# Another order for the readers of three shared PSUM tiles in a gated-delta-rule block

## The chip, the core and the metric

The kernel runs on one core of one Trainium2 chip. The metric is the device time of one execution in microseconds, lower being better. It was measured three times for the kernel before: 2231.53, 2234.38 and 2236.29 us, a median of 2234.38.

## What is computed

The reference is one transformer block on `x` of 8 sequences with 256 tokens of 256 channels, all in float32: a layer norm with per-sequence scale and shift, an attention layer whose state follows the gated delta rule, a gated residual, a second such norm, and a feed-forward layer of which only the two largest of every four hidden values are kept. The heart is the recurrence, for 16 key heads with two value heads each, all of width 128:

```python
def step(S, inp):
    q_t, k_t, v_t, b_t, d_t = inp
    Sk = jnp.einsum('bhi,bhipj->bhpj', k_t, S)
    dv = b_t[..., None] * (v_t - Sk)
    upd = jnp.einsum('bhi,bhpj->bhipj', k_t, dv)
    S = S * d_t[:, :, None, :, None] + upd
    o = jnp.einsum('bhi,bhipj->bhpj', q_t, S)
    return (S, o)
```

Its input is a projection of the tokens, convolved over four taps; its output is normalised, multiplied by a silu gate and projected back.

## The kernel before

**Tiling.** The sequences are taken in four pairs (`bp`), the key heads in groups of four (`GH`), so there are 16 groups and 64 turns of one head with one pair. The 256 tokens of a sequence are two chunks of 128 (`NCH`). Inside a chunk the recurrence is written as matrix products with the inverse of a triangular 128x128 matrix, for each of 8 systems (2 sequences, 2 chunks, 2 value heads) of a turn.

**Stages.** `prepare` makes query, values and gate of a head: products into PSUM (`ps_qv`, L432, and `ps_z`, L634), the convolution (ScalarE L418 for one tap, VectorE L420 for three more). `stage_a` and `stage_b` make keys, decays and the inverses of the 32x32 blocks for the next group; they run in the background. `levels` puts the 32x32 inverses together to 128x128 in two levels, 64 times in all. `attend` does the recurrence for one head and one sequence, 128 times in all. `shares` multiplies by the output weights (`ps_y`, L890). `feed_forward` of a finished pair of sequences fills in beside the next pair, and the last pair's runs alone at the end.

**The order of the work.** The stages are Python generators that the main loop steps in turn, which gives the program order. The tile framework then makes each engine's queue: a scheduler with a timing simulation of its own (`schedule_with_timeline_sim=True`) may move instructions past each other where no dependency forbids it. So an edit of a few lines can move instructions on every engine for the whole length of the kernel. Each engine runs its own queue strictly in order, and semaphores tie the queues together.

**Shared tiles.** A PSUM tile is one bank. The pools are `ps_in` (3 banks), `ps_inv` (2) and `ps_mix` (3). Two readers of one tile on different engines are put in program order: the later one gets a semaphore wait on the earlier one, although both only read. Readers on the same engine need no such wait. A bank is given to the next tile when its last reader is done. Three tiles matter here.

- `ps_t` in `levels` (products at L705). ScalarE evicts one half of it with a minus sign into `tt` (L712, partitions 64 to 95), VectorE transposes the other half into `low` (L714, partitions 0 to 31), ScalarE copies `low` twice into `x_top` (L720), and evicts the untransposed half last (L726). A DMA on SyncE's queue (L718) moves rows that L712 wrote into `low_up`. TensorE needs `x_top` at L731 and L734, and `low_up` at L745, one step later.
- `ps_kq` in `attend` (L779 to L783). VectorE makes the masked scores `aq` (L785), then ScalarE the two copies of `cross` (L793). TensorE needs `cross` for `ps_ks` (L806) and `aq` for `ps_o` (L824) and later for the second `ps_o` (L836).
- `ps_ks` in `attend` (L806). For each of the two value heads VectorE makes `rr` (L811) and ScalarE a part of the output `o` (L819), in turn: `rr`, `o`, `rr`, `o`. TensorE needs both `rr` for the second `ps_u` (L830). The `o` is wanted only at L837, by VectorE.

Between these, ScalarE copies of `ps_u` to `u` (L800 and L832) feed the next products directly.

## Time and profile before

| what | value |
|---|---|
| median of three runs | 2234.38 us |
| the profiled execution's own time | 2234.34 us |
| its span, first to last instruction | 2232.6 us |
| around the span | 1.7 us |
| TensorE matmul (PE) busy | 2093.5 us |
| TensorE weight loads (PEld) busy, beside the matmuls | 1643.0 us |
| VectorE (DVE) busy | 1675.3 us |
| ScalarE (ACT) busy | 1366.9 us |
| GpSimd (POOL) busy | 367.1 us |
| mean granted TensorE clock | 0.982 |

The profile names for each group of instructions the line, the engine, the tile written and the tiles read. A row of the waits reads "engine, tile and line that waited <- who ended the wait: us in total, times, longest". Matmuls are pipelined and their ends are modelled, so busy time of PE is an upper estimate of its work. Idle time of an engine counts only if TensorE, or another engine at the end of the chain, waits for it.

By stretches, PE is busy 103.1 us of the first 120 us, 1935.8 us of the 2050 us up to 2170 us, and 54.6 us of the last 62.6 us, in which the last pair's feed-forward runs by itself.

### The profile page before, as it was taken

What the parts mean: (1) busy time and instruction counts of PE and PEld (TensorE: products, weight loads), DVE (VectorE), ACT (ScalarE), POOL (GpSimd) and SP (SyncE); (2) the same over time, 40 slices, a digit from 0 to 9 for tenths busy, and PEclk for the clock granted to TensorE, in tenths of its full rate; (3) what the DMA queues carried; (4) which work ended last, traced back from release to release, by engine and by line L of the source; (5) the groups of instructions that cost most, each with busy time, mean ns of one, the idle gap of its engine ahead of it and who ended that gap; (6) DMA issues with size and microseconds to landing.
All of it is one profiled execution on the core that took longest, in us unless ns stands there. A gap on an engine that the chain in (4) does not pass through costs nothing. (4 is left out here: it accounts for less than half of the span.)

```text
span 2232.6 us, 46262 instructions
## 1 busy us (share of the span) xinstructions
PE 2093.5 (94%) x16684; PEld 1643.0 (74%) x16684; DVE 1675.3 (75%) x4039; ACT 1366.9 (61%) x4551; POOL 367.1 (16%) x375
## 2 busy tenths in 40 slices
PE   8899989899999999999999999999999999999998
PEld 5576767677677777777777777777778777777787
DVE  6687676886868696885968778686886869678547
ACT  3586666766656656665666666565665566666552
POOL 3120211212120211211111120221212012120010
PEclk9999999999999999999999999999999999999999
DMA  4332323323233433424333342433424243332336
GB/s 138 87 107 62 101 70 87 89 80 95 81 98 95 117 107 98 118 75 122 104 102 111 115 110 87 114 93 100 128 78 119 76 127 107 105 101 80 77 96 208
DMA packets 324515, 226.83 MB, mean 102 GB/s; under 512 B 254520, under 2 KB 266168, under 8 KB 324288
## 3 DMA queue, kind: packets, MB, share of 16 engines
q1 hardware_dynamic: 304416, 163.34, 27.4%
q10 hardware_dynamic: 19872, 60.54, 8.4%
q8 instruction: 133, 2.18, 0.4%
q14 instruction: 94, 0.77, 0.1%
HBM read 186.28 MB, written 29.12 MB: 96 GB/s over the span
## 5 line engine op out<-in xcount | busy, mean ns | idle before, releaser
L420 DVE SCALAR_TENSOR_TENSOR cv<-ps_qv,conv_sb,cv 128x510 f32<-128x510 f32 (+2 forms) x564 | 413.6, 738 | 72.3 <-ACT cv L418 69.2
L432 PE MATMUL ps_qv<-h_bp,wh 128*128 128x512 f32 x768 | 372.8, 610 | 5.2 <-DVE cv L420 2.5
L105 POOL TENSOR_TENSOR rs<-ss,minus_halves 128x4 f32<-128x4 f32 x128 | 137.6, 1076 | 1111.4 <-DVE ss L847 1107.7
L634 PE MATMUL ps_z<-wh,h_bp 128*128 128x256 f32 x1024 | 254.0, 391 | 6.9 <-ACT junk L451 3.8
L890 PE MATMUL ps_y<-wo,og_p 128*128 128x256 f32 x1024 | 238.8, 383 | 1.9 <-ACT o L819 1.9
L432 PEld LDWEIGHTS ps_qv<-h_bp,wh 128*128 128x128 f32 x768 | 135.3, 194 | 111.8 <-issue 99.2
L634 PEld LDWEIGHTS ps_z<-wh,h_bp 128*128 128x128 f32 x1024 | 190.3, 196 | 36.1 <-ACT junk L451 6.1
L890 PEld LDWEIGHTS ps_y<-wo,og_p 128*128 128x128 f32 x1024 | 189.4, 191 | 29.1 <-ACT o L819 2.2
L844 ACT ACTIVATE junk<-o 128x128 f32<-128x128 f32 x512 | 153.4, 303 | 78.6 <-DVE o L837 74.0
L592 DVE TENSOR_TENSOR tmp<-blk,xb 128x30 f32<-128x30 f32 (+14 forms) x480 | 157.1, 327 | 34.0 <-ACT xb L586 25.0
L551 DVE TENSOR_TENSOR_SCAN e<-dbc,diag 128x1032 f32<-128x1032 f32 x60 | 138.1, 2302 | 48.8 <-POOL diag L516 42.6
L516 POOL TENSOR_TENSOR diag<-consts,bk 128x1032 f32<-128x1032 f32 x64 | 122.9, 1920 | 307.5 <-DVE bk L507 305.8
L418 ACT ACTIVATE cv<-ps_qv,conv_sb 128x512 f32<-128x512 f32 x188 | 129.6, 691 | 67.9 <-PE ps_qv L432 67.0
L860 DVE SCALAR_TENSOR_TENSOR og<-o,rs,gz 128x128 f32<-128x128 f32 x512 | 145.1, 345 | 30.8 <-POOL rs L105 29.2
L598 DVE TENSOR_TENSOR xb<-xb,tmp 128x30 f32<-128x30 f32 (+14 forms) x480 | 156.9, 327 | 10.1
L420 DVE SCALAR_TENSOR_TENSOR k_t<-ps_k,conv_sb,k_t 128x510 f32<-128x510 f32 (+1 forms) x189 | 139.3, 738 | 23.9 <-ACT k_t L418 20.7
L806 PEld LDWEIGHTS ps_ks<-u,cross 128*128 128x128 f32 x1024 | 129.6, 193 | 15.2 <-issue 9.1
L819 ACT ACTIVATE o<-ps_ks,g_in 128x128 f32<-128x128 f32 x256 | 91.5, 367 | 80.0 <-DVE rr L811 78.4
L806 PE MATMUL ps_ks<-u,cross 128*128 128x128 f32 x1024 | 138.9, 279 | 0.7 <-DVE y L901 0.5
L190 PE MATMUL ps_ff<-h,w_ff 128*128 128x128 f32 x1024 | 128.4, 278 | 10.9 <-issue 7.4
L190 PEld LDWEIGHTS ps_ff<-h,w_ff 128*128 128x128 f32 x1024 | 120.9, 192 | 22.8 <-issue 15.2
L432 PE MATMUL ps_k<-h_bp,wk 128*128 128x512 f32 x256 | 123.5, 607 | 1.8 <-ACT junk L451 1.4
(177 smaller groups left out, 4345.4 us busy)
## 6 DMA issues: line engine op xcount, KB each, us to landing
wh<-in_w_heads ACTq DMA_DIRECT2D x64, 640.0 KB, 4.0
w_ff<-in_w_ff SPq DMA_DIRECT2D x128, 256.0 KB, 3.1
dbc<-d_dram SPq DMA_DIRECT2D x60, 516.0 KB, 3.8
wo<-in_w_heads ACTq DMA_DIRECT2D x32, 512.0 KB, 3.7
w_dn<-in_w_down SPq DMA_DIRECT2D x64, 256.0 KB, 3.1
wk<-in_w_keys SPq DMA_DIRECT2D x16, 512.0 KB, 3.2
scr<-a_t SPq DMA_DIRECT2D x256, 32.0 KB, 2.1
blk<-scr SPq DMA_DIRECT2D x16, 512.0 KB, 3.7
```

The costliest lines, as they stand in the source:

```text
L105: nc.gpsimd.tensor_tensor(out=out, in0=in_, in1=minus_halves[:, :n], op=ALU.pow)
L190: nc.tensor.matmul(ps[:, a, l, :], lhsT=w[:, k, l, :], rhs=h2[:, k, :], start=(k == 0), stop=(k == CC - 1),)
L420: nc.vector.scalar_tensor_tensor(out=dst[:, :, d:], in0=ps[:, :, : T - d], scalar=taps[:, KC - 1 - d : KC - d], in1=dst[:, :, d:], op0=ALU ...
L432: nc.tensor.matmul(ps.rearrange("p b t -> p (b t)"), lhsT=w[k], rhs=h_bp[:, k, :], start=(k == 0), stop=(k == CC - 1),)
L551: nc.vector.tensor_tensor_scan(e.rearrange("p i s t -> p (i s t)"), dbc.rearrange("p i f -> p (i f)"), diag.rearrange("p s t -> p (s t)"), ...
L592: nc.vector.tensor_tensor(out=tmp, in0=blk[:, j, j + 1 :, None].to_broadcast([P, m, j]), in1=xb[:, j, None, 0:j].to_broadcast([P, m, j]), ...
L598: solved = nc.vector.tensor_tensor(out=xb[:, j + 1 :, 0:j], in0=xb[:, j + 1 :, 0:j], in1=tmp, op=ALU.subtract)
L634: nc.tensor.matmul(ps[:, n, :], lhsT=h_bp[:, k, i * T + n * P : i * T + (n + 1) * P], rhs=wh[:, k * 640 + 384 : (k + 1) * 640], start=(k = ...
L806: nc.tensor.matmul(ps_ks[:, ct, h, :], lhsT=cross[:, h, ct, :], rhs=u0[:, h, :], start=True, stop=True)
L844: nc.scalar.activation(junk, o[:, n, h, :], AF.Square, accum_out=ss[:, n, h : h + 1])
L860: nc.vector.scalar_tensor_tensor(out=og[:, n, h, :], in0=o[:, n, h, :], scalar=rs[:, 2 * n + h : 2 * n + h + 1], in1=gz[:, i, n, h, :], op ...
L890: nc.tensor.matmul(ps_y[:, n, :], lhsT=og_p[:, j // 2, i, n, j % 2, :], rhs=wo[:, j // 2, j % 2, :], start=(j == 0), stop=(j == 3),)
```

## The change

Three pairs of statements change places. Nothing is added to or taken from the computation; no tile, pool or size changes.

```diff
@@ levels
-            nc.scalar.activation(tt[even[1], :, odd[1]], ps[even[1]], AF.Copy, scale=-1.0)
             low = mixp.tile([Q, NP, Q], F32, tag="low", name="low", bufs=1)
             nc.vector.transpose(
                 low.rearrange("p s t -> p (s t)"),
                 ps[even[0]].rearrange("p s t -> p (s t)"),
             )
+            nc.scalar.activation(tt[even[1], :, odd[1]], ps[even[1]], AF.Copy, scale=-1.0)
             nc.sync.dma_start(out=low_up[0 : 2 * Q], in_=tt[2 * Q :, NS:, 2 * Q :])
@@ attend
+            cross = two.tile([P, 2, 2, P], F32, tag="cross", name="cross")
+            for h in range(2):
+                nc.scalar.activation(cross[:, h], ps_kq[:, 1:3], AF.Copy, scale=e[:, i, h, P:PE1])
             aq = two.tile([P, NCH, 2, P], F32, tag="aq", name="aq")
             nc.vector.tensor_tensor(
                 out=aq,
...
-            cross = two.tile([P, 2, 2, P], F32, tag="cross", name="cross")
-            for h in range(2):
-                nc.scalar.activation(cross[:, h], ps_kq[:, 1:3], AF.Copy, scale=e[:, i, h, P:PE1])
             yield
@@ attend
                     op0=ALU.mult,
                     op1=ALU.add,
                 )
+            for h in range(2):
                 nc.scalar.activation(
                     o[:, 1, h, :], ps_ks[:, 0, h, :], AF.Copy, scale=g_in[rec["bp"]][:, i, h0 + h : h0 + h + 1]
                 )
```

After it, `low` reads `ps_t` ahead of L712's eviction, and the DMA of L718 still follows that eviction; both copies of `cross` read `ps_kq` ahead of `aq`; both `rr` read `ps_ks` ahead of both `o`. Of the built program, the queues differ on every engine over the whole length. TensorE's queue falls into 3304 runs of equal instructions, where it had 3331.

## The prediction

> **What bounds the kernel.** I read the page first, then the waits of TensorE, then all waits, then one stretch of the timeline.

> ```profile
> span 2232.6 us, 46262 instructions
> PE 2093.5 (94%) x16684; PEld 1643.0 (74%) x16684; DVE 1675.3 (75%) x4039; ACT 1366.9 (61%) x4551; POOL 367.1 (16%) x375
> ...
> PE   8899989899999999999999999999999999999998
> ...
> PEclk9999999999999999999999999999999999999999
> ```

> TensorE sets the time: busy 94% in every slice, at nearly its full clock. It does the same products after the change, so the change can act only on its idle time, 2232.6 - 2093.5 = 139.1 us, and on how its queue is ordered. Adding up all rows of TensorE's waits by the engine that ended them, 83 us are ended by ACT, 23 by DVE, 18 by DMAs. These rows touch the three tiles:

> ```profile
> PE ps_gt L876 <- ACT cross L793: 13.5, 9, 3.1
> ...
> PE ps_w L731 <- ACT x_top L720: 5.1, 4, 2.2
> ...
> PE ps_u L798 <- ACT cross L793: 3.5, 3, 2.2
> ...
> PE ps_w L731 <- ACT t_inv L726: 2.1, 6, 0.6
> ...
> PE ps_y L890 <- ACT o L819: 1.9, 2, 0.9
> ...
> PE ps_t L745 <- DMA low_up<-t_inv: 1.2, 1, 1.2
> ...
> PE ps_u L830 <- ACT o L819: 0.6, 1, 0.6
> ...
> PE ps_u L830 <- DVE rr L811: 0.2, 1, 0.2
> ```

> Without the DMA they are 13.5 + 5.1 + 3.5 + 2.1 + 1.9 + 0.6 + 0.2 = 26.9 us, 1.2% of the span: the most that the edits can win directly. `ps_gt` and `ps_u` read no `cross`; they wait because `cross` is the last reader of the bank that they take over. The rest of what the tiles cost lies on ACT and DVE (all waits):

> ```profile
> ACT o L819 <- DVE rr L811: 78.4, 93, 4.1
> ...
> DVE cv L420 <- ACT cv L418: 69.2, 61, 3.9
> ...
> ACT x_top L720 <- DVE low L714: 47.9, 27, 4.9
> ...
> DVE low L714 <- ACT t_inv L712: 22.5, 21, 3.9
> DVE rr L811 <- ACT o L819: 21.6, 32, 1.4
> ...
> ACT cross L793 <- DVE aq L785: 17.2, 17, 4.3
> ...
> ACT u L800 <- PE ps_u L798: 13.4, 13, 2.4
> ```

> Here engines wait for a reader of the same bank, not for data. The timeline shows how such a chain runs (start, duration, engine; idle time in brackets):

> ```profile
> 2160.80 0.35 DVE L811 SCALAR_TENSOR_TENSOR rr<-ps_ks,g_ex,vn 128x128 f32<-128x128 f32 x1 [3.02 <-PE ps_ks L806]
> ...
> 2161.18 0.37 ACT L819 ACTIVATE o<-ps_ks,g_in 128x128 f32<-128x128 f32 x1 [1.41 <-DVE rr L811]
> ...
> 2161.58 0.35 DVE L811 SCALAR_TENSOR_TENSOR rr<-ps_ks,g_ex,vn 128x128 f32<-128x128 f32 x1 [0.43 <-ACT o L819]
> ```

> `rr` ends at 2161.15, `o` starts at 2161.18, ends at 2161.55, and the second `rr` starts at 2161.58: a hand-over costs 0.03 us, and the second `rr`, which TensorE needs, is 0.43 us late for an `o` that nobody needs yet.

> **Part by part.** No instruction is added or removed, so busy times stay; waits move.

> *Both `rr` first.* From the end of `ps_ks` to the second `rr` the least was 0.04 + 0.34 + 0.03 + 0.37 + 0.03 + 0.34 = 1.15 us (means of L811 and L819: 340 and 367 ns) and becomes 0.04 + 2 x 0.34 = 0.72. In the queues of the two built programs the waits of `o` on DVE fall from 256 to 128 and those of `rr` on ACT from 128 to none. Directly TensorE can win the 1.9 + 0.6 + 0.2 = 2.7 us of `ps_y` and `ps_u` (L830), of which `ps_y` waits for a bank whose last reader stays `o`. I take half: **-1.4**, bounds 0 and -2.7. The remaining `o` wait comes 0.34 us later in the chain, so I count half of the 78.4 us of ACT as freed: 39.

> *`cross` first.* `cross` now waits for the products alone, which frees 17.2 us of ACT. From `ps_kq` to the second `cross` the least falls from 0.04 + 0.68 + 0.03 + 2 x 0.49 = 1.73 to 1.02 us; to `aq` it rises from 0.72 to 1.02 + 0.03 + 0.68 = 1.73. In TensorE's order at least 3.4 us of other products lie between `ps_kq` and the `ps_o` that needs `aq`, and 12.7 at the median, so the later `aq` costs nothing by itself; without that cover it would be 1.0 us in each of 128 turns. The bank is given back after all three readers as before, now by DVE. Of the 17.0 us in which TensorE waited for that bank, I take a quarter as won, nearer to nothing, because the chain to the bank's release is as long as it was: **-4.2**, bounds -17.0 and, where DVE's queue is the later one, about the same the other way, +17.0.

> *ACT freed.* 39 + 17.2 = 56 of ACT's idle 850 us (2232.6 - 1366.9, less what lies below the threshold of a wait) go. TensorE's ACT-ended waits outside the three tiles are 83 - 27 = 56 us. In proportion, 56/850 x 56: **-3.7**, bounds 0 and twice that.

> *DVE.* Its waits for `rr` (21.6) and `low` (22.5) go, 44 us. New are the waits of `aq` for `cross`. The nearest row is DVE reading behind ACT in `ps_qv`: 69.2 us over 188 such pairs, so 47 us over 128. At the other end all 128 wait the whole pair, 130 us. I take 47, which cancels the 44: **0**. Behind a waiting `aq` in DVE's queue stand convolutions (L420), which give `ps_in` banks back to TensorE; at 130 us, TensorE's 23 us of DVE-ended waits grow in proportion to DVE's 554 idle us by 86/554 x 23 = 3.6, or threefold if convolutions bear it all, +11.

> *`low` first.* ACT's queue has L712, L720, L720, L726 in this order before and after. The two chains to `x_top` are 0.04 + 0.375 + 0.03 + 0.43 + 0.03 + 0.62 and 0.04 + 0.43 + 0.03 + 0.375 + 0.62: the same but 0.03 us. Only `low` is earlier, and L712 is 0.47 us later with all that depends on it: the DMA of L718, queued on SP, which lands 2.2 us after its issue. TensorE waited for it once (1.2 us) and it has a whole step of `levels` as cover, so **+1**; all 64 uncovered would be 64 x 0.47 = +30. Behind it on SP stand mostly the transfers of the next turn's `x_top` (35 of 64), which have a whole turn, some 35 us (2232.6/64), and wait 0.47 us longer. DVE's 22.5 us go, ACT's 47.9 move from L720 to L712.

> The 22.5 us of `low` waiting for L712 are a row of this case. [...]

> *TensorE's order.* The scheduler moves products on the whole length. I compared the four links in which one ACT copy stands between two products, `u`, second `u`, `w1` and `w2`, by the products that lie between, at the spacing of the trace (0.111 us for 128 columns, 0.434 for 512). The least hop is 0.03 + 0.37 + 0.03 = 0.43 us; with one ACT instruction of 0.5 ahead 0.95. Links with less cover than that, before and after: first `u` to `ps_ks` 3 and 11 of 128, second `u` to `ps_o` 20 and 16 of 128, `w1` 3 and 1 of 64, `w2` 6 and 1 of 64. The missing cover adds up to 12.2 us before and 9.3 after: **-3**; with hops of 1.5 us 32.1 and 29.0, again -3. The first `u` alone gets worse, by 3 to 10 us; the others win 6 to 13. Fewer runs in the queue (3331 to 3304) at 139/3331 us of idle each are 1 us, within this.

> Sum: -1.4 - 4.2 - 3.7 + 0 + 1 - 3 = -11.3. The profiled execution took 2234.34 us, which is the median of the runs (2234.38). So **2223.0 us**.

> **Rivals.**
> 1. *More is won* (0.12). All 26.9 us and the freed ACT's 3.7 go: 2203.7. For it: the waits of TensorE are long (3.1 us) where ACT's head is blocked. Against: of 27 us, 7.2 hang on a chain (`x_top`) that is not shortened.
> 2. *Nothing to be measured* (0.19): the ACT waits were idle time that nobody needed, and only +1 and -3 remain, or `aq` takes on DVE what ACT got free (-11.3 + 11): 2232 to 2234. For it: TensorE waits for `rr` only 0.2 us in all.
> 3. *Slower, through the first `u`* (0.27). 28 of 128 copies have under 1.5 us of products as cover, where 10 had; ACT stood ready for this copy only 13 times of 128, so it usually has others ahead. If hops are 1.5 us and the gains on the other links and banks stay on paper, it is 2234.3 + 9.7 = 2244; hops of 2 us cost 18.2 and make it 2252. It decides from hops of 1.2 us on (5.2 us), if nothing else is won.

> **How the numbers follow.** The forecast has 0.42, the rivals 0.12, 0.19 and 0.27. A difference of 0.2% (4.5 us) is about what a measurement of this kernel can tell from no change. Faster by more: 0.42 + 0.12 = 0.54; within: 0.19; slower: 0.27. The forecast's own range is 2216 to 2230. The range to be held 8 times in 10 goes from the most that can be won, 2204, to rival 3 with hops of 2 us, 2252; what lies beyond on either side, such as `low_up` uncovered in all turns, I give under 2 in 10.

> **What would show it.** Right: the row of `o` waiting for `rr` falls to about half, those of `rr` for `o`, `cross` for `aq` and `low` for L712 are gone; a row of `aq` waiting for `cross` appears with some 50 us; PE's idle time is some 11 us less, with `ps_gt` <- `cross` replaced by a smaller row. ACT's wait at L720 turns into one at L712 of like size. Wrong: PE waits for `u` or `w` of over 10 us, `aq` waiting for over 100 us with `ps_qv` waiting for `cv`, or `ps_t` (L745) waiting for the DMA in many turns. A granted clock other than 0.98 would move the time by itself and would have to be taken out first.

## The result and the profile after

The changed kernel took 2275.51 us (median of 5 runs, 2271.46 to 2276.57), the kernel before 2233.97 us beside it (5 runs): a ratio of 1.0184, 95% interval 1.0169 to 1.0198. It is 1.8% slower. The forecast, 2223.0 us with 2204 to 2252, was wrong in sign and in range.

The page of the kernel after, its span and its sums (lines behind L818 are one higher than before; the moved statements are now at L713, L717, L786 and L788):

```profile
span 2274.8 us, 46446 instructions
...
PE 2109.9 (93%) x16684; PEld 1649.2 (72%) x16684; DVE 1680.2 (74%) x4039; ACT 1352.9 (59%) x4549; POOL 374.1 (16%) x375
```

The span is 42.2 us longer: TensorE is idle for 164.8 us where it was 139.1 (+25.7), and it is busy for 16.4 us more with the same 16684 products. The second part is the clock. The mean granted clock fell from 0.982 to 0.974. In the clock records it drops to 0.5 for pieces of 3.41 or 6.83 us: 22 pieces before, 27 after. Within the span that is 81.9 and 117.7 us at half speed, so 41.0 and 58.9 us lost. Busy time less that loss is 2052.6 before and 2051.0 after. This profile has the lowest clock of the five runs: the other four show 0.977 and 0.978, which is some 50 to 52 us lost, so the clock's part there is 9 to 11 us in place of 17.9. Two stretches of equal length, before and then after (start and end, length, busy time of PE, PEld, DVE, ACT, POOL with counts, PEclk, DMA share, GB/s), show the loss on the whole length:

```profile
500.00:1000.00 500.00, 474.29 (x3796) 372.87 (x3795) 391.93 (x932) 314.03 (x1080) 85.47 (x85) 0.99 0.35 97
1000.00:1500.00 500.00, 474.35 (x3948) 376.41 (x3946) 383.69 (x900) 304.02 (x1028) 83.68 (x82) 0.99 0.39 109
```

```profile
500.00:1000.00 500.00, 467.31 (x3792) 365.63 (x3792) 376.02 (x885) 299.78 (x1034) 85.90 (x82) 0.98 0.34 95
1000.00:1500.00 500.00, 472.81 (x3844) 371.18 (x3842) 376.32 (x872) 300.61 (x1042) 85.99 (x83) 0.98 0.37 104
```

PE is busy for less of both stretches and at a slightly lower clock. The same products of `attend` (`ps_kq`, `ps_ks`, `ps_o`) come 7 to 9 us late at 500 us, 16 at 1000, 29 to 35 at 1500 and 40 at 2100. So the loss has no one place; it gathers over the whole length.

TensorE's waits, before and then after:

```profile
PE ps_z L634 <- ACT junk L451: 3.8, 7, 0.8
...
PE ps_qv L432 <- DVE cv L420: 2.5, 4, 1.1
...
PE ps_out L244 <- DMA w_dn<-in_w_down: 2.1, 3, 1.2
...
PE ps_u L798 <- ACT og_p L877: 1.4, 3, 0.5
```

```profile
PE ps_u L798 <- ACT og_p L878: 13.3, 12, 1.6
PE ps_out L244 <- DMA w_dn<-in_w_down: 12.7, 8, 4.6
PE ps_qv L432 <- DVE cv L420: 11.9, 7, 3.6
PE ps_z L634 <- ACT junk L451: 11.4, 8, 1.9
PE ps_gt L877 <- DVE aq L788: 9.8, 13, 1.4
```

The row of `ps_gt` waiting for `cross` (13.5) is replaced by a smaller one, for `aq` (9.8), as forecast. What grew stands on other tiles. `junk` (L451) is a sum of squares by ScalarE over `ps_n2q` or `ps_n2k`, banks of the pool `ps_in` that `ps_z` and `ps_qv` also use; `og` is the gated output that VectorE makes, `ps_gt` its transpose by TensorE and `og_p` ScalarE's copy of that. By the engine that ended them, TensorE's waits for ACT fell from 83.3 to 72.0 us, those for DVE rose from 23.1 to 56.1 and those for DMAs from 18.4 to 27.9.

All waits after, the rows of the three tiles:

```profile
ACT t_inv L717 <- DVE low L713: 61.7, 24, 6.0
...
ACT o L820 <- DVE rr L811: 44.5, 39, 3.9
...
ACT t_inv L717 <- DVE rstd L134: 35.6, 6, 7.0
...
DVE aq L788 <- ACT cross L786: 12.5, 26, 1.1
```

`o` for `rr` fell from 78.4 to 44.5; the rows of `rr` for `o`, `cross` for `aq` and `low` for L712 are gone; `aq` waits for `cross` for 12.5 us in all. The eviction, now at L717, waits for `low` and also sits behind `rstd`, other work of VectorE. So on its own tiles the change did what was forecast, at a lower price in waits, and the time was lost elsewhere.

### The profile page after: what moved, and what is told of

The parts are those of the page before. It is cut to its first block, busy times and chain, and to the rows that moved or that the text cites. A ratio compares the mean times of both kernels' runs of the same rounds, so it can differ in the third digit from the quotient of the medians.

```text
span 2274.8 us, 46446 instructions
## 1 busy us (share of the span) xinstructions
PE 2109.9 (93%) x16684; PEld 1649.2 (72%) x16684; DVE 1680.2 (74%) x4039; ACT 1352.9 (59%) x4549; POOL 374.1 (16%) x375
## 2 busy tenths in 40 slices
PE   8899989899999999999999999999999999999998
## 5 line engine op out<-in xcount | busy, mean ns | idle before, releaser
L420 DVE SCALAR_TENSOR_TENSOR cv<-ps_qv,conv_sb,cv 128x510 f32<-128x510 f32 (+2 forms) x564 | 413.3, 738 | 83.8 <-ACT cv L418 80.2
L432 PE MATMUL ps_qv<-h_bp,wh 128*128 128x512 f32 x768 | 372.4, 609 | 15.3 <-DVE cv L420 11.9
L105 POOL TENSOR_TENSOR rs<-ss,minus_halves 128x4 f32<-128x4 f32 x128 | 144.6, 1130 | 1061.6 <-DVE ss L848 1060.7
L634 PE MATMUL ps_z<-wh,h_bp 128*128 128x256 f32 x1024 | 261.2, 398 | 26.7 <-ACT junk L451 11.4
L592 DVE TENSOR_TENSOR tmp<-blk,xb 128x30 f32<-128x30 f32 (+14 forms) x480 | 156.4, 326 | 38.2 <-ACT xb L586 29.5
L418 ACT ACTIVATE cv<-ps_qv,conv_sb 128x512 f32<-128x512 f32 x188 | 129.0, 688 | 93.1 <-PE ps_qv L432 92.7
L420 DVE SCALAR_TENSOR_TENSOR k_t<-ps_k,conv_sb,k_t 128x510 f32<-128x510 f32 (+1 forms) x189 | 138.8, 736 | 33.6 <-ACT k_t L418 32.0
L806 PEld LDWEIGHTS ps_ks<-u,cross 128*128 128x128 f32 x1024 | 130.1, 192 | 18.5 <-issue 9.6
L806 PE MATMUL ps_ks<-u,cross 128*128 128x128 f32 x1024 | 139.8, 278 | 1.1
L772 ACT ACTIVATE vn<-ps_v,nk 128x256 f32<-128x256 f32 x256 | 108.3, 474 | 18.6 <-PE ps_v L767 17.7
```

Of the source, the lines that this page charges most:

```text
L105: nc.gpsimd.tensor_tensor(out=out, in0=in_, in1=minus_halves[:, :n], op=ALU.pow)
L420: nc.vector.scalar_tensor_tensor(out=dst[:, :, d:], in0=ps[:, :, : T - d], scalar=taps[:, KC - 1 - d : KC - d], in1=dst[:, :, d:], op0=ALU ...
L432: nc.tensor.matmul(ps.rearrange("p b t -> p (b t)"), lhsT=w[k], rhs=h_bp[:, k, :], start=(k == 0), stop=(k == CC - 1),)
L592: nc.vector.tensor_tensor(out=tmp, in0=blk[:, j, j + 1 :, None].to_broadcast([P, m, j]), in1=xb[:, j, None, 0:j].to_broadcast([P, m, j]), ...
L634: nc.tensor.matmul(ps[:, n, :], lhsT=h_bp[:, k, i * T + n * P : i * T + (n + 1) * P], rhs=wh[:, k * 640 + 384 : (k + 1) * 640], start=(k = ...
L806: nc.tensor.matmul(ps_ks[:, ct, h, :], lhsT=cross[:, h, ct, :], rhs=u0[:, h, :], start=True, stop=True)
```

## The experiments

Two theories stood against each other; the expectations name them R and Q (two more, P and I, are told in theirs). **R (readers):** one of the new orders of readers costs by itself, above all `aq` behind `cross`. **Q (queues):** the edit only makes the scheduler write other queues, and these happened to be worse; any edit could do so. Each ratio is to the kernel before on the same chip, with its 95% interval.

### One order of queues, the other order of readers

The first four kernels hold each engine's queue to the order that the other kernel's has, by ordering edges without a semaphore between neighbours of a queue (those that float keep only their own dependencies):

```diff
+        for a, b in zip(queue, queue[1:]):
+            tc.add_manual_dep(b, a.name, NoSync, reason="queue")
```

`e1_old_queues`: the statements of after, the queues of before; only `o` and L717 float.

> The changed kernel's statements, so the three tiles are read in the new order, but the queues of TensorE, VectorE, GpSimd and SyncE are held to those of the kernel before, and ScalarE's too but for the 256 `o` and the 64 evictions of L712, which may float. Theory Q (the loss of 42 us comes from the queues that the scheduler made anew, not from the readers): 2215 to 2238 us, that is the prediction's own -11 or nothing; TensorE's idle about 125 to 140 us. Theory R (the readers' new order itself costs, banks coming free later and `aq` holding VectorE's queue): 2265 to 2276 us with the old queues as well.

Measured: 2399.03 us, 1.0755 [1.0731, 1.0779]. Its waits:

```profile
DVE aq L788 <- ACT cross L786: 204.8, 103, 5.9
...
PE ps_gt L877 <- DVE og L861: 68.7, 36, 4.2
```

`aq` keeps its early place in DVE's queue and must now wait there for `cross`, with the rest of that queue behind it: 204.8 us, in place of the 12.5 of the changed kernel, where the scheduler was free to move it.

`e2_new_queues`: the statements of before, the queues of after; `o`, `aq` and L712 float.

> The other corner: the statements of the kernel before, so the tiles are read in the old order, but the queues held to those of the changed kernel, only `o`, `aq` and the eviction of L712 floating. Theory Q: 2262 to 2295 us, the loss stays although the readers stand as before (or grows, since these queues were not made for them). Theory R: 2230 to 2245 us, the loss goes with the readers.

Measured: 2387.47 us, 1.0703 [1.0681, 1.0724]. Here it is the second `rr` that stands too early for its reader order:

```profile
DVE rr L811 <- ACT o L819: 99.8, 127, 2.9
```

Both times lie far above what either theory expected. Both show that an order of readers and a queue belong together, and neither weighs R against Q. So all readers of the three tiles (`o`, `rr`, `aq`, `cross`, `low`, the eviction) were left to float in the next two.

`e9_old_queues_free_readers`: the statements of after, the queues of before but for the readers.

> As the first run with held queues, but all readers of the three tiles (`o`, `rr`, `aq`, `cross`, `low` and L712) may float on ScalarE and VectorE; all else is held to the queues of the kernel before. In that first run `aq` was held at its old place and made VectorE wait 205 us for `cross`. Theory P (a reader needs its own place in its engine's queue, and the first run held it in the wrong one): most of the 168 us go, 2225 to 2280 us, with `aq` waiting under 60 us. Theory Q (the loss of the whole change comes from TensorE's and the other queues): 2215 to 2245 us. Theory R (the readers' order itself costs): 2260 us or more.

Measured: 2248.99 us, 1.0083 [1.0053, 1.0113].

`e10_new_queues_free_readers`: the statements of before, the queues of after but for the readers.

> The other corner again: the statements of the kernel before, all readers of the three tiles free, all else held to the queues of the changed kernel. Theory P: far below the 2387 us of the run that held `rr` too, since `rr` no longer waits for `o` with the queue held. Theory Q: 2260 to 2295 us. Theory R: 2225 to 2250 us.

Measured: 2322.39 us, 1.0412 [1.0379, 1.0445]. In before's queues the kernel with the new readers is 0.8% slower than the kernel before. In after's queues it is the old order that is worse, by 1.0412 / 1.0184 = 2.2% against the changed kernel. So queues fit the readers that they were written for. The first came between the range of Q (to 2245 us) and that of R (from 2260), as the third theory of its text, P, had it (2225 to 2280, `aq` waiting for under 60 us: it waited for 10.4); the second came above Q's and R's. How the 1.8% divides between R and Q these two don't show: no kernel was run that is held to its own queues, so what the holding itself costs is unknown.

### Each part alone, and in pairs

Each kernel has one or two of the three hunks shown in the change, and nothing else.

```diff
 e3: cross ahead of aq                   (hunk 2)
 e4: both rr ahead of both o             (hunk 3)
 e5: low ahead of the eviction           (hunk 1)
 e11: hunks 2 and 3;  e13: hunks 1 and 3;  e14: hunks 1 and 2
```

> `cross` ahead of `aq` alone, queues as the scheduler makes them. Theory R: this part frees its bank by VectorE and holds VectorE's queue, so it should carry most of the loss: 2260 to 2276 us. Theory Q: any value within some 2% of 2234 us, above or below, with no relation to the whole change.

> Both `rr` ahead of both `o` alone. Theory R: it only removes waits, so 2225 to 2236 us. Theory Q: any value within some 2% of 2234 us; if it is 1% slower, a part that only removes waits has lost time through the queues.

> `low` ahead of the other half's eviction alone. Theory R: the chain to `x_top` is as long as before and `low_up` comes 0.47 us later, so 2230 to 2245 us. Theory Q: any value within some 2% of 2234 us, and the three single parts need not add up to the 42 us of the whole.

> Two parts together, `cross` ahead of `aq` and both `rr` ahead of both `o`, without `low`. Alone they gave 1.0038 and 0.9970 of the time before. If parts add up: 1.0008, 2236 us. If the loss of the whole change is a matter of these two together (theory R, by interaction): 1.015 or more, 2267 us. Theory Q: within some 2%, unrelated.

> `low` first and both `rr` first, without `cross`. Alone they gave 0.9977 and 0.9970. If parts add up: 0.995, 2220 us. Theory I (the loss needs `low` together with `rr`): 1.010 or more. Theory Q (each set of queues has its own time): within 0.985 to 1.015, unrelated to the sum.

> `low` first and `cross` first, without `rr`. Alone they gave 0.9977 and 1.0038. If parts add up: 1.0015, 2234 us. Theory I (the loss needs `low` together with `cross`): 1.010 or more. Theory Q: within 0.985 to 1.015, unrelated to the sum.

| kernel | parts | us | ratio |
|---|---|---|---|
| e3 | cross | 2237.61 | 1.0038 [1.0026, 1.0050] |
| e4 | rr | 2221.82 | 0.9970 [0.9956, 0.9984] |
| e5 | low | 2225.87 | 0.9977 [0.9961, 0.9992] |
| e13 | low, rr | 2219.44 | 0.9941 [0.9917, 0.9965] |
| e11 | cross, rr | 2243.05 | 1.0061 [1.0041, 1.0082] |
| e14 | low, cross | 2259.74 | 1.0118 [1.0073, 1.0164] |
| after | all three | 2275.51 | 1.0184 [1.0169, 1.0198] |

Without `cross` the parts gain and add up: 0.9970 x 0.9977 = 0.9947, measured 0.9941. Every kernel with `cross` is slower than before. The two gaining parts no longer gain beside it: `rr` gives 1.0061 / 1.0038 = 1.0023, which is within its bound of 1 (0.0024), `low` 1.0118 / 1.0038 = 1.0080. Theory R missed three times here: it had expected e3 to carry most of the loss (2260 us or more), and e4 and e5 came below the ranges that it gave them. TensorE's waits in e3:

```profile
PE ps_gt L876 <- DVE og L860: 20.4, 12, 2.7
PE ps_gt L876 <- DVE aq L788: 17.9, 18, 1.5
...
PE ps_qv L432 <- DVE cv L420: 8.0, 10, 2.2
```

In e3 all of TensorE's waits for ACT fall to 43.8 us (from 83.3), those for DVE rise to 69.2 (from 23.1), and its idle time stays at 139.3 us. With `cross` alone TensorE waits for DVE in place of ACT, for as long as before; in this profile the 7.1 us more are the clock (48.5 us lost, from 41.0).

For `rr` and `low` alone, the rows of their own tiles, e4 and then e5:

```profile
ACT o L820 <- DVE rr L811: 52.2, 63, 3.1
```

```profile
ACT t_inv L717 <- DVE low L713: 72.2, 27, 7.5
```

In e4 `o` waits 52.2 us (78.4 before). TensorE's idle time stays at 140.8 us; its busy time falls by 15.0 to 2078.5, of which 6.9 are clock (34.1 us lost, from 41.0). So the time that `rr` won in this profile is not idle time of TensorE, and 8.1 us of it are not the clock either; where they come from is open.

### Edits that should do nothing

To see how far queues alone scatter, statements of one engine were exchanged that have the same size and change no order between engines: L748 and L749 (e6, e12, e16 to e18), L699 and L700 (e7, e15), and the heads of `og` (e8).

```diff
 e6 (t2)
-            nc.scalar.activation(tt[top, 0:NS, bottom], ps[top], AF.Copy, scale=-1.0)
             nc.scalar.activation(tt[top, NS:, bottom], ps[bottom], AF.Copy, scale=-1.0)
+            nc.scalar.activation(tt[top, 0:NS, bottom], ps[top], AF.Copy, scale=-1.0)
 e7 (w1)
-            nc.scalar.copy(w1[odd[0]], ps[odd[0]])
             nc.scalar.copy(w1[odd[1]], ps[odd[1]])
+            nc.scalar.copy(w1[odd[0]], ps[odd[0]])
 e8
             for n in range(NCH):
-                for h in range(2):
+                for h in (1, 0):
                     nc.vector.scalar_tensor_tensor(
                         out=og[:, n, h, :],
 e12: the whole change and t2;  e15: the whole change and w1;  e16: hunk 3 and t2
 e17: hunk 2 and t2;  e18: hunks 1 and 3 and t2
```

> A neutral edit of the kernel before: the last two ScalarE evictions of `levels` (L748, L749) change places. Both are on one engine, of one size and needed together, and no reader of the three tiles moves; but the scheduler makes other queues on every engine. Theory Q: it moves the time too, by up to 2% either way. Theory R: 2230 to 2238 us.

> A second neutral edit: the two ScalarE copies to `w1` in `levels` (L699, L700) change places. Theory Q: moves the time by up to 2% either way, not by the same as the first neutral edit. Theory R: 2230 to 2238 us.

> A third neutral edit: the two value heads of `og` on VectorE (L860) are taken in the other order. Theory Q: moves the time by up to 2% either way. Theory R: 2230 to 2238 us.

> The whole change with the first neutral edit on top (L748 and L749 change places), so the same reader order with another set of queues. Theory Q: the loss is that of one set of queues, so the ratio moves clearly from 1.018, most likely down, to between 0.995 and 1.012. Theory R: 1.013 to 1.020, the neutral edit's own -0.5% and the change's +1.8%.

> The whole change with the second neutral edit on top (L699 and L700 change places); alone that edit gave 0.999. Its queues lie closer to those of the changed kernel than with the first neutral edit. Theory Q: the ratio moves off 1.018 by 0.3% or more. Theory R (the readers' order costs 1% or more whatever the queues): 1.010 to 1.020.

> A candidate that might beat both kernels: both `rr` first (0.9970 alone) with the first neutral edit (0.9947 alone), neither of which adds a wait. If parts add up: 0.992, 2212 us. Theory Q: they don't; between 0.985 and 1.010.

> Cross ahead of aq, with the two statements L748 and L749 of the same engine in the other order. Theory R (the order of cross and aq costs by itself): the neutral swap alone measured 0.9947 and cross alone 1.0038, so it is slower than the neutral swap alone: 0.998 or more, 2230 us or more. Theory Q (it only fell upon poor queues): 0.990 to 0.997, some 2218 us, and as often below the neutral swap as above it.

> Low ahead of the eviction, both rr ahead of both o, and the neutral swap; cross after aq as before. If parts without cross add up: 0.9941 x 0.9947 = 0.989, some 2209 us. If the scatter of neutral edits rules: anything from 0.985 to 1.000.

| kernel | edit | us | ratio |
|---|---|---|---|
| e6 | t2 | 2221.37 | 0.9947 [0.9927, 0.9967] |
| e7 | w1 | 2229.99 | 0.9990 [0.9980, 1.0000] |
| e8 | heads of `og` | 2241.21 | 1.0047 [1.0028, 1.0065] |
| e12 | all three, t2 | 2253.68 | 1.0094 [1.0066, 1.0122] |
| e15 | all three, w1 | 2271.06 | 1.0170 [1.0139, 1.0201] |
| e16 | rr, t2 | 2210.56 | 0.9896 [0.9864, 0.9928] |
| e17 | cross, t2 | 2230.87 | 1.0004 [0.9991, 1.0018] |
| e18 | low, rr, t2 | 2201.67 | 0.9870 [0.9851, 0.9889] |

An edit that changes no order between readers on different engines moves this kernel by up to 0.5% either way, which is 11 us and as much as the whole forecast. But it is not noise: t2 gives 0.9947 alone, 0.9926 beside `rr` (0.9896 / 0.9970), 0.9929 beside `low` and `rr`, 0.9966 beside `cross`, 0.9912 beside all three; w1 gives 0.9990 alone and 0.9986 beside all three. So the name "neutral" was wrong for it; why it gains was not studied. The same division for `cross` (the bound is the root of the sum of the two half-intervals' squares):

| `cross` ahead of `aq`, added to | factor |
|---|---|
| nothing | 1.0038 +- 0.0012 |
| t2 | 1.0057 +- 0.0024 |
| rr | 1.0091 +- 0.0025 |
| low | 1.0141 +- 0.0049 |
| low, rr, t2 | 1.0227 +- 0.0034 |
| low, rr | 1.0244 +- 0.0029 |

Six times out of six it costs, and most beside both other parts; a second set of queues (t2) gives the same within the bounds. The two smallest factors are no larger than what e8 gave for nothing (1.0047), but the other four are clear of it. If poor queues were an accident, one would expect factors on both sides of 1, and others with t2. So Q in the form that any edit could have done it is unlikely: in this kernel `cross` ahead of `aq`, with the queues that the scheduler writes for it, is the slower order. `low` and `cross` together (e14) came where its text puts a loss by the two together (1.010 or more). One expectation spoke the other way: e12 (1.0094) came into the range given to Q (0.995 to 1.012) and not into R's (from 1.013), because t2 gains more beside the whole change than alone.

### How it costs, as far as the traces show

From the records I took, for each PSUM tile, the time from the end of its last product to the end of each reader. The table has means over all tiles (128 `ps_kq`, 64 `ps_n2k`, 63 `ps_k`).

| us from the last product | before | e3 | after | e13 | e12 | e18 |
|---|---|---|---|---|---|---|
| `cross` (each copy) | 3.88 | 2.27 | 2.00 | 3.51 | 1.90 | 3.35 |
| `aq` | 2.02 | 4.21 | 4.01 | 2.03 | 3.86 | 1.70 |
| both done, bank given back | 4.09 | 4.21 | 4.01 | 3.69 | 3.86 | 3.54 |
| `junk` on `ps_n2k` | 7.93 | 9.74 | 9.82 | 8.27 | 9.94 | 8.71 |
| `k_t` on `ps_k` (DVE) | 4.23 | 3.82 | 5.42 | 4.25 | 5.32 | 3.88 |

`cross` and `aq` exchange places. In five of the six pairs that differ in `cross` alone, the bank comes back 0.1 to 0.3 us later (before and e3: 4.09 to 4.21; e13 and after: 3.69 to 4.01; e18 and e12: 3.54 to 3.86); beside t2 alone it comes back 0.3 us sooner (4.18 to 3.85), and that pair costs 0.57% all the same. So the bank's return does not carry the price.

What also gets later is the background work on `ps_in`. In the seven kernels with `cross` whose queues are the scheduler's own (after, e3, e11, e12, e14, e15, e17) the norms' `junk` ends 9.3 to 10.0 us after its products, in the nine without (before, e4 to e8, e13, e16, e18) 6.8 to 9.1, and it is later in each of the six pairs. The keys' convolution `k_t` ends after 5.3 to 5.4 us where all three parts are in (after, e12, e15), otherwise after 3.7 to 4.8. This goes with the queues, not with the readers: e9 (after's readers, before's queues) has 8.1 and 4.4 us, e10 (before's readers, after's queues) 10.0 and 5.4. But later norms alone do not make a kernel slow: e6 and e16, without `cross`, have 9.1 and 8.9 us and ratios of 0.9947 and 0.9896.

The products of `ps_z` come later in every pair. To count it, I took the distance from each product's start to the next one's, less the median of such distances after products of the same shape, where it is positive. Summed over `ps_z`, `cross` adds 9 us to nothing, 11 to t2, 5 to rr, 18 to low, 24 to low, rr and t2, and 39 to low and rr, each from one profile. This too goes with the queues: 22 us before, 17 in e9, 49 in e10 and after (50 in e1, where `aq` holds up VectorE).

One of the things that `ps_z` waits for is `junk`. The tile view of `ps_z` counts how long TensorE, its weight loads and the copy `gz` sat idle before an instruction of `ps_z` until `junk` ended (us, times); in before, after, e12 and e13 in this order:

```profile
  ACT junk L451: 10.0, 15
```

```profile
  ACT junk L451: 25.0, 18
```

```profile
  ACT junk L451: 19.0, 12
```

```profile
  ACT junk L451: 3.3, 6
```

Between e13 and after it rises from 3.3 to 25.0; e18 has no such row, e12 has 19.0. But it is not the price: with `cross` alone it falls from 10.0 to 8.0 us (e3), and the largest of the kernels with the scheduler's own queues, 28.8, stands in e17, whose ratio is 1.0004.

The pair of e18 and then e12, which differ in `cross` alone, shows the whole sum:

```profile
span 2203.9 us, 46326 instructions
...
PE 2082.2 (94%) x16684; PEld 1637.6 (74%) x16684; DVE 1657.4 (75%) x4039; ACT 1363.6 (62%) x4552; POOL 364.1 (17%) x375
```

```profile
span 2252.9 us, 46425 instructions
...
PE 2101.5 (93%) x16684; PEld 1637.3 (73%) x16684; DVE 1687.8 (75%) x4039; ACT 1355.0 (60%) x4550; POOL 376.4 (17%) x375
```

The span is 49.0 us longer, 29.8 of it idle time of TensorE and 19.3 busy time. Of the latter only 1.7 are the clock (41.0 us lost, then 42.7). The other 17.6 us are busy time that the clock does not explain; by tile the largest differences are `ps_gt` (65.1 to 70.9 us, less the clock) and `ps_z` (225.9 to 230.0). The ends of products are modelled in the profile (in `ps_z` of the kernel before a product's record lasts 379 ns at the median, and at the full clock the next starts after 216), so waiting may hide in them; that is not settled. By the same count of starts as above, `ps_z` is 23.6 us later in all (12.3 to 36.0), `ps_u` at L798 13.5, `ps_w` at L731 11.5 and `ps_gt` 11.1; `ps_ff` is 20.2 earlier. The waits behind the last reader of the bank of `ps_kq`, the direct price of the new order, are 3.8 + 1.8 = 5.6 us in e18 and 10.5 in e12 (e18, then e12):

```profile
PE ps_u L798 <- ACT cross L793: 3.8, 3, 3.3
...
PE ps_gt L877 <- ACT cross L793: 1.8, 2, 1.2
```

```profile
PE ps_u L798 <- ACT og_p L878: 14.5, 11, 2.1
PE ps_gt L877 <- DVE aq L788: 10.5, 12, 1.4
PE ps_z L634 <- ACT junk L451: 8.7, 5, 1.7
```

So it is shown that `cross` first, with the queues written for it, costs; that the waits for its own bank carry little of it (4.9 of the 49.0 us here); and that in the queues written for it the norms and `ps_z` come later. That the later `ps_z` is the main link is argued from these rows; no run moved it alone. It also stays open why `low` and `rr` make `cross` dearer.

**The best version.** Leaving `cross` where it was and keeping the rest with t2 (e18) took 2201.67 us, 0.987 of the kernel before: 28.7 us less in the profile, 17.4 of it idle time of TensorE.

## Why the prediction was wrong, by its steps

- **The change acts on idle time alone.** Half right. 25.7 us of the 42.2 are idle time, but 17.9 are the clock, which no term priced. The prediction wanted the clock taken out first; that leaves some 24 us slower, so the sign stands. In three kernels more clock was lost beside the longer idle time: 17.9 / 25.7 = 0.7 us for each further idle microsecond here, 0.5 in e1 and 0.4 in e10, all against the kernel before. In the traces of before and after TensorE was busy for 0 to 78% of the 3.41 us ahead of a drop, where 93 to 94% is the mean.
- **Both `rr` first, -1.4**, with its 39 of the 56 us of ACT freed, -2.6. Alone it measured (0.9970 - 1) x 2234 = -7 us (-3 to -10). Right in sign, and `o` for `rr` fell from 78.4 to 52.2 us. The mechanism is not confirmed: the term stood for idle time of TensorE, which did not fall (139.1 to 140.8 us). The gain is also no larger than that of t2, though it repeats beside `low` (0.9941 / 0.9977 = 0.9964) and t2 (0.9949).
- **`cross` first, -4.2.** This step failed, and with it the sum. It took the waits for the bank of `ps_kq` for the whole price. On that bank it was near: in no kernel with `cross` first and free queues does `ps_o` wait for `aq`; the chain to the bank's release is as long as it was (4.09 and 4.21 us in e3); and the 17.0 us of waits became 17.9 + 0.9 = 18.8 in e3 and 9.8 + 1.1 = 10.9 in after, inside its bounds. But the part measured +8 us alone (1.0038) and +54 us beside the other two (1.0244 of 2219). What it had at nothing is what the queues written around the new order do to tiles that the change does not touch, `ps_z` above all.
- **ACT freed, -3.7.** ACT's end of TensorE's waits did fall by 11 us, the three tiles' own included, but DVE's rose by 33.
- **DVE, 0.** The row came smaller than forecast: `aq` waits for `cross` for 12.5 us, not 47; `aq` itself ends 2 us later (2.02 to 4.01). TensorE's waits behind DVE grew by 33 us, three times the upper end (+11), though DVE waited so little. But this does not mark the loss: in e18, the fastest kernel, they are 52.6 us, and with `rr` alone 46.5, where they were 23.1.
- **`low` first, +1.** Alone it measured (0.9977 - 1) x 2234 = -5 us, again within what edits that should do nothing give. The forecast rows came: the wait of `low` is gone and ACT's is at L717 (61.7 us, 47.9 at L720 before); `ps_t` did not wait for `low_up` in many turns. Beside `cross` and `rr` the same part costs 1.0184 / 1.0061 = 1.2%.
- **TensorE's order, -3.** For the links it counted it came out: by the count of starts, the products behind them go from 40.8 to 38.2 us, that is -2.6 (`ps_ks` 6.8 to 8.1, the second `ps_o` 6.8 to 8.3, `ps_t` 13.9 to 11.3 and 13.3 to 10.5). But these four links were not where the new order of the queues told: `ps_z` is 27.3 us later in all (21.8 to 49.1), `ps_out` 12.2, `ps_u` at L798 12.0 and `ps_qv` 8.5, and none of them was counted.
- **Summing.** The terms were added as if they were independent. Those of `low` and `rr` are; with `cross` the three parts together cost 2% more than their product (0.9970 x 0.9977 x 1.0038 = 0.9985, against 1.0184).
- **The rivals.** Rival 3 had the sign (0.27), but by a mechanism that did not happen, and its 2244 and 2252 are short of 2275. Of the marks in "Wrong" little was there: `ps_qv` waiting for `cv` rose from 2.5 to 11.9 us and the clock was 0.974, but `aq` waited for 12.5 us and not over 100, and no wait of TensorE for `u` or `w` comes near 10 us. The range left no room for scatter by the scheduler, which by e6 to e8 alone is 11 us to either side.
- **A reading of rows.** "Here engines wait for a reader of the same bank, not for data" holds for `o`, `rr`, `cross` and `low` in that list. `x_top` behind `low` (47.9 us), the three taps of `cv` behind the first (69.2) and `u` behind `ps_u` (13.4) are waits for data. The 69.2 were also the base for the 47 us of `aq`. And TensorE is not busy for 94% "in every slice": five of the forty digits are 8.

## What to carry to other kernels

Where a scheduler writes the queues, an order of readers is not priced by its own waits: take the parts one by one and in pairs, beside one or two edits that should do nothing, before believing a sum of a few tenths of a per cent. Here it cost to change which engine gives a bank back last (`cross` and `aq`). The waits for that bank hardly changed (4.9 of the 49.0 us from e18 to e12), and the price appeared on other tiles, in the queues written around it (`ps_z` comes 23.6 us later there). In a kernel at 94% of TensorE, count the granted clock as a term beside the idle time: it was 17.9 of the 42.2 us here.

## What was not expected of the hardware

Within `ps_z` of the kernel before, products follow each other by 216 ns at the full clock and by 427 at half. The records of single products stretch less regularly: 27 of the 28 that lie wholly in such a piece took 634 ns, one 796, where the median of all is 379 (least, median and longest, first and last start):

```profile
L634 PE MATMUL ps_z<-wh,h_bp x1024: 377/379/796, 73.9 to 2130.3; 128*128 128x256 f32 x171
```
